# A graph network of three layers: the next layer's products over its first eight source pairs, dealt between the steps of a layer's last four tiles

## The chip, the cores and the metric

The kernel runs on one core of one Trainium2 chip, in one launch. The metric is the device time of a run in microseconds (us); less is better. The engines of the core work side by side, each through its own instructions in order: TensorE (PE, with PEld for its weight loads), VectorE (DVE), ScalarE (ACT), GpSimd (POOL) and SyncE (SP), which here only issues transfers. PE writes to PSUM, 16 DMA engines move the data.

## The reference

```python
src, dst = edge_index[0], edge_index[1]          # 200000 edges, sorted by dst
h = jnp.maximum(_layernorm(x, axis=-1), 0.0)     # x: 6250 x 128, float32

def _sage_conv(x, src, dst, Wl, bl, Wr):
    agg = jax.ops.segment_max(x[src], dst, num_segments=x.shape[0])
    agg = jnp.where(jnp.isfinite(agg), agg, 0.0)
    return agg @ Wl + bl + x @ Wr

h = jax.nn.leaky_relu(_sage_conv(h, src, dst, Wl1, bl1, Wr1), 0.01)   # 128 -> 256
h = jax.nn.leaky_relu(_sage_conv(h, src, dst, Wl2, bl2, Wr2), 0.01)   # 256 -> 256
h = jax.nn.leaky_relu(_sage_conv(h, src, dst, Wl3, bl3, Wr3), 0.01)   # 256 -> 128
return x + h
```

Each layer takes, for every node, the elementwise maximum over the rows of its in-edges' sources, and puts that and the node's own row through two products. Destinations are drawn with the square of a uniform number, so low node numbers have many edges and high ones few.

## The kernel before

**Tiles and pairs.** The nodes lie in 50 tiles of 127. As sources the tiles are taken two at a time: 25 pairs, `g` from 24 down to 0, a pair's features being 512 KB in layers 1 and 2 and 256 KB in layer 0 (the features stand there in two parts, whose products are summed). As destinations they are cut into five groups `k`: 0 has 24 narrow tiles (few edges), 1 has 11 wide tiles, 2 has 8 virtual tiles (the three tiles with the most edges, spread over more rows, with eight extra planes), 3 has 8 wide tiles, 4 has the last 4 narrow tiles.

**Products.** For a pair and a destination tile, one edge per destination row (wide tiles: one from each tile of the pair) is fetched by a product with a one-hot matrix. `one_hot` makes these on ACT: in layer 0 from the edge list (L916) and stores them in a compact form for later (`far`, L922), then the float form (L920); later layers load `far` and need only L920. `products` (L939) issues the PE work of a **step**, `maxima` (L954, L956) takes the result on DVE into an accumulator `acc` in SBUF. In layers 1 and 2 a step is four tiles of 128 columns: eight products of 512 columns on PE, and one maximum of 1024 elements per row on DVE for narrow tiles, two for wide ones. A source pair is six steps for group 0, three wide ones for group 1 (the third of 384 columns), two wide and two narrow ones for group 2, two wide ones for group 3 and one narrow one for group 4. In layer 0, with half the features, a step is eight tiles.

**Lists.** The edges that no one-hot serves stand in four lists. A list is worked off by **gathers** of 128 rows (`Listed.gather`, L988: an indirect DMA issued by POOL, and behind it a small memset L992 that spaces them), with an index made by ACT (`release`, L977) and the maxima on DVE (`maximum`, L1003 and L1008). `CAPS` has the gathers of each list: 147, 91, 228 and 47, 513 per layer. The last list belongs to group 4. Gathers of a layer read the table of all nodes' rows, so they start only when the last node of the layer before is done.

**Nodes.** A tile that has all its maxima becomes a `Node`: `fetch` (L1033, the list's result, an indirect DMA by POOL), `merge` (transposes on PE L1049, maximum on DVE L1055), `linear` (products L1060, L1062, L1064 on PE, copy L1066 on ACT), `rows` (L1073), `turn` (transposes of the new row block L846 to L851) and `rest` (L856). The virtual tiles first go through `Joined`: eight fetches, eight merges (L1112, L1114), a scan, eight `send`s (transposes L1124, copy L1126 into one buffer `joined_v`, a store), and then three nodes.

**Order.** Everything is written out by hand, step by step. A planner first lists the steps:

```python
PASSES = (((0,), (1,), (2,), (3,), (4,)), ((0, 1), (2, 3), (4,)), ((0, 1), (2, 3), (4,)))
```

so layer 0 goes through its groups one by one, 25 pairs each, and layers 1 and 2 have three passes over the pairs: groups 0 and 1 together (225 steps), groups 2 and 3 (150 steps), group 4 (25 steps). Then it puts every gather, maximum and node stage at a step of an `agenda`; in each step the stages of that step are issued between the two halves of its products. Gathers of lists 0 to 2 are spread evenly from the layer's first steps (`rows_at`) to the end of group 3, those of list 3 over the last pass. The nodes of groups 0 and 1 come at every third step of the second pass, those of group 3 and the virtual ones in the last pass, one per step, and the four of group 4 after it, in the next layer's first steps. The preparation of lists 1 to 3 and of the one-hots (`chores`: `mask_rows`, `flag_rows`, `pick_rows`, `rank_rows`, `expand`, `lookups`, all DVE) lies in steps 0 to 172 of layer 0. Pairs are loaded two orders ahead into three buffers (`load_pair`), one-hots are made up to six ahead (`make_hots`).

Of the kernel before, what the change touches and what calls it, by code (L numbers as in the profile page):

```python
# [42 lines left out]
P = 128  # L43
# [16 lines left out]
)  # L60
DEEP = (24, 24, 48, 24)
NA = 8
WINDOW = (48, 64)
# [6 lines left out]
def kernel(ctx: ExitStack, tc: tile.TileContext, x, src, dst,  # L70
# [33 lines left out]
    PASSES = (((0,), (1,), (2,), (3,), (4,)), ((0, 1), (2, 3), (4,)), ((0, 1), (2, 3), (4,)))  # L104
# [6 lines left out]
    LISTS = (GROUPS[0], GROUPS[1], GROUPS[2] + GROUPS[3], GROUPS[4])  # L111
# [32 lines left out]
    GB = (1, 1, 1, 1, 5)  # L144
# [802 lines left out]
    def maxima(step, s, p, acc):  # L947
        layer, k, g, (c, w, _, odd_u), _ = step
        if widths[layer] // P == 2:
            of, to = p[:, :, :w], acc[:, :, c * P : c * P + w]  # L950
        else:
            of, to = p.rearrange("p h c -> p (h c)")[:, :w], acc[:, 0, c * P : c * P + w]
        if g == NG - 1 and c == step[3][2] and (odd_u is None or s == 0):
            nc.vector.tensor_copy(to, of)  # L954
        else:
            nc.vector.tensor_max(to, to, of)  # L956
# [188 lines left out]
    steps, begins, ends_at, order, blocks, jobs_h = [], [], {}, [], [], []  # L1145
    for layer in range(3):
        begins.append(len(steps))
        for n, ks in enumerate(PASSES[layer]):
            for g in range(NG - 1, -1, -1):
                order.append((layer, n, g))  # L1150
                of = {}
                for k, (c0, pw, odd), cs in parts_in(layer, ks):
                    if k not in of:
                        if (NG - 1 - g) % GB[k] == 0:
                            blocks.append((layer, k, list(range(g, g - GB[k], -1))))
                        of[k] = max(i for i, b in enumerate(blocks) if b[:2] == (layer, k))
                    jobs_h += [(len(steps), of[k], (layer, k, g, c0, pw, odd, s)) for s in range(2)]
                    for c in cs:
                        steps.append((layer, k, g, c, n))
                        ends_at[layer, k] = len(steps)  # L1160
    begins.append(len(steps))
# [21 lines left out]
    EXTRA_OF = GROUPS[VIRT]  # L1183

    def late_rows(k):
        us = LISTS[k]
        i0 = 0
        for part in [[u for u in us if (u in EXTRA_OF) == v] for v in (True, False)]:
            if not part:
                continue  # L1190
            chores.append((2.5, lambda part=part: mask_rows(part, S_acc)))
            chores.append((18 if part[0][0] == "w" else 6, lambda part=part: flag_rows(part, S_acc)))
            for i in range(0, len(part), 4):
                chores.append((7, lambda k=k, i0=i0 + i, p=part[i : i + 4]: pick_rows(k, i0, p, S_acc)))
# [31 lines left out]
    stops.append((len(chores), 52, 104))  # L1226
    for s in range(2):
        late_lookups(GROUPS[3], s)
    stops.append((len(chores), 104, 140))
    late_rows(3)  # L1230
    late_lookups(LISTS[3], 0)
    stops.append((len(chores), 140, 172))
# [7 lines left out]
    i0 = 0  # L1240
# [8 lines left out]
    for layer in range(3):  # L1249
        b0, end = begins[layer], begins[layer + 1]  # L1250
        lists_ = [early_list if (layer, k) == (0, 0) else Listed(layer, k) for k in range(NL)]
        early = 0 if layer else EARLY
        turn = ends_at[layer, 3] - DELAY[layer]
        whens = []
        for part, t0, t1 in ((lists_[:3], max(b0 + 2, rows_at), turn), (lists_[3:], turn, end - 1 - SOON)):
# [23 lines left out]
        late = 0  # L1279
# [15 lines left out]
        free = 0  # L1295
        for k in range(len(GROUPS)):
            done = done_at[LISTED[GROUPS[k][0]][0]]
            n = len(GROUPS[k])
            if k == VIRT:
                t0 = joins = max(ends_at[layer, k], done + gap) + 1  # L1300
                key = (layer, "joined")

                def start(key=key, layer=layer):
                    accs[key] = Joined(layer, accs[layer, VIRT])

                plan(t0, MAXIMA, start)
                for v in range(NV):
                    plan(t0 + v, FETCH, lambda key=key, v=v: accs[key].fetch(v))
                    plan(t0 + 2 + v, MERGE, lambda key=key, v=v: accs[key].merge(v))
                for i in range(widths[layer] // P):  # L1310
                    plan(t0 + 10, MERGE, lambda key=key, i=i: accs[key].scan(i))
                for v in range(NV):
                    plan(t0 + 11 + v // 2, TURN, lambda key=key, v=v: accs[key].send(v))
                continue
            nodes = [
                ((layer, k, "node", i), lambda layer=layer, k=k, i=i: Node(layer, k, i, accs[layer, k]))
                for i in range(n - 1, -1, -1)
            ]
            if k == len(GROUPS) - 1:
                t0 = max(end, done + 1) + 1  # L1320
                assert free <= t0
                for j, (key, make) in enumerate(nodes):
                    stages(t0, key, make, after=[d + j for d in (2, 3, 3, 4)])
                rows_at = max(late, t0 + 3 + n - 1)
                continue
            t0 = max(ends_at[layer, k], done + gap, free) + 1
            every = 1 if layer == 0 or k == 3 else 3
            for j, (key, make) in enumerate(nodes):
                stages(t0 + every * j, key, make)
            free = t0 + every * (n - 1) + 1  # L1330
            if k == VIRT + 1:
                free = max(free, joins + 17)
                for a in range(VT):
                    stages(free + a, (layer, None, a), lambda layer=layer, a=a: Node(layer, None, a, None))
                free += VT
            late = max(late, free + 4)
# [36 lines left out]
    ACC = ((0, 0), (1, 8), (1, 0), (1, 19), (0, 20))  # L1373
# [3 lines left out]
    for t in range(max(max(agenda)[0] + 1, len(steps) + 1)):  # L1377
# [4 lines left out]
        if t == begins[1]:  # L1382
# [324 lines left out]
```

## Time and profile before

| | us |
|---|---|
| three timed runs | 3393.09, 3399.34, 3400.73 (median 3399.34) |
| the profiled execution's own time | 3386.89 |
| its span in the profile | 3384.8 |
| PE busy in the span | 2535.2 (75%) |
| DVE busy | 2674.5 (79%) |
| POOL busy | 2461.2 (73%) |
| ACT busy | 1879.2 (56%) |

The profile is one execution. A view by stretches of the span gives each engine's busy time, the granted clock of PE as a share of full speed, and what the DMA engines moved. A row of the timeline has the start, the time taken, the engine, line and operation, output and inputs, shape, a count, and in brackets the idle time before it and what ended it. The rows of a chain of waits have start, length and what it was. The boundaries between passes used below are the starts of the first product of each pass, found by counting the products of L939.

### The profile page before, as it was taken

To read this page: it belongs to the slowest core of one execution; us is meant where nothing else is said; L and a number is where in the kernel's file an instruction comes from. 1 tells how busy PE (TensorE), PEld (TensorE's weight loads), DVE (VectorE), ACT (ScalarE), POOL (GpSimd) and SP (SyncE) were. 2 spreads that over 40 slices of the span, in tenths; PEclk is the share of its full clock that TensorE was granted. 3 is DMA by queue.
4 is the path that set the end of the run, shared out by engine and by line. 5 is a ranking of instruction groups with operands and counts; after the bars stand their busy time and mean duration, and the time that the engine had idled before them with its cause. 6 is when DMAs were issued, how large, how long until landed. Compare 5 with 4: busy or idle time off the path is not lost.

```text
span 3384.8 us, 38792 instructions
## 1 busy us (share of the span) xinstructions
PE 2535.2 (75%) x9920; PEld 1833.9 (54%) x9920; DVE 2674.5 (79%) x4157; ACT 1879.2 (56%) x2762; POOL 2461.2 (73%) x3478
## 2 busy tenths in 40 slices
PE   1035664365676667899999989887999999989886
PEld 1023333243454333677777666655777777666654
DVE  6677679777766653699989888884699989999974
ACT  5128897466999996555544434433455545333432
POOL 4788865476867655488888767775388888878782
PEclk9986777587778876899999999998999999999998
DMA  9234554267676677656757767667666756666575
GB/s 303 50 65 135 140 140 134 82 199 195 164 223 172 191 210 206 187 183 199 195 175 187 225 201 226 203 190 241 210 194 194 202 176 179 203 188 206 171 228 166
DMA packets 355527, 620.98 MB, mean 183 GB/s; under 512 B 68694, under 2 KB 216883, under 8 KB 354657
## 3 DMA queue, kind: packets, MB, share of 16 engines
q1 hardware_dynamic: 210561, 367.36, 33.7%
q0 software_dynamic: 79872, 199.22, 24.1%
q10 hardware_dynamic: 64864, 51.83, 4.5%
q8 instruction: 83, 1.36, 0.2%
q14 instruction: 147, 1.20, 0.1%
HBM read 476.03 MB, written 142.13 MB: 183 GB/s over the span
## 4 chain that ended last, share of the span: by engine, by line
PE 28%; DVE 22%; POOL 16%; DMA 12%; issue 11%; ACT 10%; SPq 0%; ACTq 0%; DVEq 0%; POOLq 0%
PE pg L939 21%; DVE acc L956 10%; POOL g L988 9%; ACT away L916 6%; DMA g<-table,let 5%; POOL pace_t L992 3%; ACT hot L920 3%; DVE g L1008 2%; PE z_p L1062 2%; DVE g L1003 2%; PE z_p L1064 2%; POOL picks L621 2%; DMA far<-away 1%; DMA joined<-joined_v 1%; DVE acc L557 1%
## 5 line engine op out<-in xcount | busy, mean ns | idle before, releaser
L939 PE MATMUL pg<-hot,pair_sb 128*128 128x512 f32 x8000 | 2212.9, 426 | 425.3 <-ACT hot L920 191.3
L939 PEld LDWEIGHTS pg<-hot,pair_sb 128*128 128x128 f32 x8000 | 1551.0, 204 | 950.8 <-ACT hot L920 422.2
L988 POOL DMA_INDIRECT g<-table,let x1539 | 1552.1, 1009 | 664.5 <-ACT let L977 291.0
L956 DVE TENSOR_TENSOR acc<-acc,pg 128x1024 f32<-128x1024 f32 (+3 forms) x1439 | 1642.8, 1167 | 415.0 <-PE pg L939 388.7
L920 ACT ACTIVATE hot<-idx_sb 128x1024 fp32r<-128x1024 uint8 (+1 forms) x900 | 817.1, 946 | 552.7 <-PE pg L939 349.2
L992 POOL MEMSET pace_t<- 128x300 bf16 x1539 | 563.0, 366 | 0.8
L916 ACT ACTIVATE away<-idx_sb,near 128x1024 uint8<-128x1024 uint8 (+2 forms) x450 | 463.7, 1030 | 68.4 <-DMA best<-g 17.7
L920 ACT ACTIVATE hot<-away 128x1024 fp32r<-128x1024 uint8 (+2 forms) x450 | 427.7, 950 | 46.0 <-PE pg L939 31.8
L1066 ACT COPY s<-z_p 127x256 f32<-127x256 f32 (+1 forms) x150 | 50.2, 334 | 452.0 <-PE z_p L1064 421.0
L1003 DVE TENSOR_TENSOR g<-g 128x1024 f32<-128x1024 f32 (+5 forms) x218 | 221.4, 1016 | 20.4 <-DMA g<-table,let 20.2
L1033 POOL DMA_INDIRECT agg<-best,end_i x141 | 144.7, 1026 | 106.9 <-PE aT_p L1049 41.2
L1008 DVE TENSOR_TENSOR g<-g 128x512 f32<-128x512 f32 (+3 forms) x351 | 173.1, 493 | 10.5 <-DMA g<-table,let 0.2
L1062 PE MATMUL z_p<-wr,hT_in 128*128 128x256 f32 (+1 forms) x500 | 142.9, 404 | 6.6 <-DMA hT_in<-across 6.6
L1064 PE MATMUL z_p<-wl,mz 128*128 128x256 f32 (+1 forms) x500 | 127.7, 373 | 14.6 <-DVE mz L1055 13.8
L846 PE MATMUL hT_p<-ident,h 128*128 128x128 f32 x200 | 47.9, 326 | 116.2 <-DVE mz L1055 54.1
L977 ACT ACTIVATE let<-ell 128x4 int32<-128x4 int16 (+3 forms) x444 | 81.1, 191 | 79.1 <-DMA ell<-picks 67.7
L848 ACT COPY hT<-hT_p 128x254 f32<-128x254 f32 x100 | 36.7, 367 | 141.5 <-PE hT_p L846 136.6
L1064 PEld LDWEIGHTS z_p<-wl,mz 128*128 128x128 f32 x500 | 91.8, 212 | 32.4 <-DVE mz L1055 22.3
L846 PEld LDWEIGHTS hT_p<-ident,h 128*128 128x128 f32 x200 | 24.6, 158 | 148.2 <-DVE mz L1055 67.1
L1062 PEld LDWEIGHTS z_p<-wr,hT_in 128*128 128x128 f32 x500 | 82.1, 207 | 31.4 <-issue 8.9
L1055 DVE TENSOR_TENSOR mz<-acc,aT_p 128x256 f32<-128x256 f32 (+1 forms) x141 | 52.3, 371 | 58.4 <-PE aT_p L1049 58.3
L621 POOL DMA_INDIRECT picks<-picked,to_i x55 | 57.7, 1050 | 43.0 <-DVE rank_h L597 32.6
(268 smaller groups left out, 1223.2 us busy)
## 6 DMA issues: line engine op xcount, KB each, us to landing
pair_sb<-pair SPq DMA_DIRECT2D x150, 512.0 KB
far<-away ACTq DMA_DIRECT2D x350, 128.0 KB
idx_sb<-far SPq DMA_DIRECT2D x50, 768.0 KB
pair_sb<-pair SPq DMA_DIRECT2D x125, 256.0 KB
pair<-pr SPq DMA_DIRECT2D x100, 256.0 KB
idx_sb<-far SPq DMA_DIRECT2D x50, 512.0 KB
g<-table,let POOLq DMA_INDIRECT x1539
idx_sb<-idx SPq DMA_DIRECT2D x50, 384.0 KB
```

What stands on the lines that cost most here:

```text
L621: s = nc.gpsimd.indirect_dma_start(out=picks[k], out_offset=bass.IndirectOffsetOnAxis(ap=to_i[k][:, i : i + 1], axis=0), in_=picked[k][:, ...
L916: nc.scalar.activation(away, t[:, at : at + w], AF.Abs, bias=near[:, s : s + 1], scale=1.0)
L920: nc.scalar.activation(hot[:, :w], away, AF.Relu, bias=1.0, scale=-1.0)
L939: nc.tensor.matmul(to, pr[:, s, i, kk * P : (kk + 1) * P], hot[:, o : o + bw], start=((alone or s == 0) and i == 0), stop=((alone or s == ...
L956: nc.vector.tensor_max(to, to, of)
L988: nc.gpsimd.indirect_dma_start(out=self.tiles[q, b][:, i, :], out_offset=None, in_=tables[self.layer], in_offset=bass.IndirectOffsetOnAxis ...
L992: nc.gpsimd.memset(pace_t, 0.0)
L1003: nc.vector.tensor_max(base[:, : i + 1, :], base[:, : i + 1, :], g[:, : i + 1, :])
L1008: nc.vector.tensor_max(base[:, :h, :], base[:, :h, :], base[:, w - h : w, :])
L1033: nc.gpsimd.indirect_dma_start(out=self.agg[:, : self.F], out_offset=None, in_=of, in_offset=bass.IndirectOffsetOnAxis(ap=at, axis=0),)
L1062: nc.tensor.matmul(z_p, self.hT[:, i, :], wr[layer][:, i, :], start=False, stop=False)
L1064: nc.tensor.matmul(z_p, self.m[:, i, :], wl[layer][:, i, :], start=False, stop=(i == K - 1))
```

## The change

The last pass of layers 0 and 1 is no longer 25 steps of group 4: between them stand the six group-0 steps of the next layer for each of its first eight source pairs, 48 steps, so that the pass has 73. The pairs 24 to 17 are concerned, whose tiles are nodes of group 0 and are done earlier in the layer. The next layer's first pass then starts with group 0 alone for two more pairs (`MORE`), 12 steps, goes on with groups 0 and 1 for the 15 pairs left, and the second pass takes group 1 along for the first ten pairs (9 steps a pair), then groups 2 and 3 for 15 (6 steps a pair). Group 4's accumulator moves to the place of group 1's.

With it change: the lists (list 3 now has half of group 3 and group 4, 98 gathers instead of 47; list 2 has 182 instead of 228; 518 per layer); in layer 2 all four lists are spread evenly to the end of the last pass; the nodes of groups 0 and 1 come at every fourth step in layers 1 and 2, four nodes of group 3 and the three virtual ones at every third; the other four nodes of group 3 come with those of group 4 after the last pass, eight instead of four; group 4's one-hot inputs are loaded pair by pair instead of five pairs at once; and the chores for list 3 stand earlier, all chores ending at step 156.

```diff
-    (47, 24, 20, 17, 16, 15, 14, 13, 12, 12, 11, 10, 8, 6, 2, 1),
-    (23, 10, 8, 6),
+    (47, 24, 19, 17, 15, 14, 13, 12, 10, 8, 2, 1),
+    (31, 15, 12, 11, 9, 8, 7, 5),
 )
-DEEP = (24, 24, 48, 24)
+DEEP = (24, 24, 48, 32)
+OVER, MORE = 8, 2
...
-    LISTS = (GROUPS[0], GROUPS[1], GROUPS[2] + GROUPS[3], GROUPS[4])
+    LISTS = (GROUPS[0], GROUPS[1], GROUPS[2] + GROUPS[3][:4], GROUPS[3][4:] + GROUPS[4])
...
-    GB = (1, 1, 1, 1, 5)
+    GB = (1, 1, 1, 1, 1)
...
+    back, walks = list(range(NG - 1, -1, -1)), []
     for layer in range(3):
+        if layer == 0:
+            body = [(n, g, (k,)) for n, k in enumerate((0, 1, 2, 3)) for g in back]
+        else:
+            late_g = back[: OVER + MORE]
+            body = [(0, g, (0,)) for g in back[OVER : OVER + MORE]] + [(0, g, (0, 1)) for g in back[OVER + MORE :]]
+            body += [(1, g, (1, 2, 3) if g in late_g else (2, 3)) for g in back]
+        walks += [(layer, *w) for w in body]
+        last = [((i + 0.5) / NG, layer, 4, g, (4,)) for i, g in enumerate(back)]
+        if layer < 2:
+            last += [((i + 0.6) / OVER, layer + 1, 0, g, (0,)) for i, g in enumerate(back[:OVER])]
+        walks += [w[1:] for w in sorted(last)]
...
+        spans = ((lists_[:3], begin_at, turn), (lists_[3:], turn, end - 1 - SOON))
+        if layer == 2:
+            spans = ((lists_, begin_at, end - 1 - SOON),)
...
+        every = 1 if layer == 0 else 4
+        for k in (0, 1):
+            for i in range(len(GROUPS[k]) - 1, -1, -1):
+                t = max(t, ready(k, i))
+                stages(t, *node_of(k, i))
+                t += every
...
+        t0 = max(t, end, done_at[3] + 1) + 1
+        lasts = [(4, i) for i in range(3, -1, -1)] + [(3, i) for i in range(7, 3, -1)]
+        for j, (k, i) in enumerate(lasts):
+            f = max(0, j - 2)
+            stages(t0 + f, *node_of(k, i), after=[d + j - f for d in (2, 3, 3, 4)])
...
-    ACC = ((0, 0), (1, 8), (1, 0), (1, 19), (0, 20))
+    ACC = ((0, 0), (1, 8), (1, 0), (1, 19), (1, 8))
...
-        if t == begins[1]:
+        if t == done_with_fields:
             making.close()
             fields.close()
```

More of the change, by code (lines that the diff above doesn't have):

```diff
@@ L1143, in parts_in @@
         return [p[1:] for p in sorted(parts, key=lambda p: p[:2])]
-    steps, begins, ends_at, order, blocks, jobs_h = [], [], {}, [], [], []
+    steps, begins, ends_at, order, blocks, jobs_h = [], {}, {}, [], [], []
+    back, walks = list(range(NG - 1, -1, -1)), []
     for layer in range(3):
[L1147 to L1160, printed above, removed]
@@ new lines @@
+        if layer < 2:
+            last += [((i + 0.6) / OVER, layer + 1, 0, g, (0,)) for i, g in enumerate(back[:OVER])]
+        walks += [w[1:] for w in sorted(last)]
+    first_g = {}
+    for layer, n, g, ks in walks:
+        order.append((layer, n, g))
+        of = {}
+        for k, (c0, pw, odd), cs in parts_in(layer, ks):
+            first_g.setdefault((layer, k), g)
+            if k not in of:
+                blocks.append((layer, k, [g]))
+                of[k] = len(blocks) - 1
+            jobs_h += [(len(steps), of[k], (layer, k, g, c0, pw, odd, s)) for s in range(2)]
+            for c in cs:
+                begins.setdefault(layer, len(steps))
+                steps.append((layer, k, g, c, n))
+                ends_at[layer, k] = len(steps)
@@ L1181, with runs_of @@
     here_now, listed_at = [0], {0: 0}
-    EXTRA_OF = GROUPS[VIRT]
+    def runs_of(us):
+        cuts = [i for i in range(1, len(us)) if us[i] != (us[i - 1][0], us[i - 1][1] + 1)]
+        return list(zip([0] + cuts, cuts + [len(us)]))
     def late_rows(k):
@@ L1293, in stages @@
                 plan(ta + d, rank, lambda stage=stage: getattr(accs[key], stage)())
[L1295 to L1336, printed above, removed]
@@ new lines, in ready, with node_of @@
+        def ready(k, i):
+            return max(ends_at[layer, k], done_at[LISTED[GROUPS[k][i]][0]] + gap) + 1
+        def node_of(k, i):
+            return (layer, k, "node", i), lambda layer=layer: Node(layer, k, i, accs[layer, k])
+        t = 0
+        every = 1 if layer == 0 else 4
[4 more added lines that the diff above has]
+                t += every
+        assert t + 5 < ends_at[layer, VIRT]
@@ new lines, with start @@
+        joins = max(ready(VIRT, 0), t)
+        key = (layer, "joined")
+        def start(key=key, layer=layer):
+            accs[key] = Joined(layer, accs[layer, VIRT])
+        plan(joins, MAXIMA, start)
+        for v in range(NV):
+            plan(joins + v, FETCH, lambda key=key, v=v: accs[key].fetch(v))
+            plan(joins + 2 + v, MERGE, lambda key=key, v=v: accs[key].merge(v))
+        for i in range(widths[layer] // P):
+            plan(joins + 10, MERGE, lambda key=key, i=i: accs[key].scan(i))
@@ new lines @@
+        for v in range(NV):
+            plan(joins + 11 + v // 2, TURN, lambda key=key, v=v: accs[key].send(v))
+        every = 3
+        for i in range(3, -1, -1):
+            t = max(t, ready(3, i))
+            stages(t, *node_of(3, i))
+            t += every
+        t = max(t, joins + 17)
+        for a in range(VT):
+            stages(t, (layer, None, a), lambda layer=layer, a=a: Node(layer, None, a, None))
+            t += every
+        t0 = max(t, end, done_at[3] + 1) + 1
+        lasts = [(4, i) for i in range(3, -1, -1)] + [(3, i) for i in range(7, 3, -1)]
```

31 lines of the change are left out of this document (16 added, 15 removed).

## The prediction, on record before the changed kernel ran

> **What bounds the kernel now.** First the page, for the whole span:
>
> ```profile
> span 3384.8 us, 38792 instructions
> PE 2535.2 (75%) x9920; PEld 1833.9 (54%) x9920; DVE 2674.5 (79%) x4157; ACT 1879.2 (56%) x2762; POOL 2461.2 (73%) x3478
> PEclk9986777587778876899999999998999999999998
> ```
>
> No engine is full, and the clock is low only in the first 40%, layer 0. These are means over stages, so next the view by stretches, cut at the passes: layer 0's group 3 and group 4, then for layer 1 and layer 2 each the steps in which the last nodes of the layer before end (9 steps), the rest of the first pass (24 pairs), the second pass (25 pairs), the last pass (25 steps), and the tail.
>
> ```profile
> core 0: us, PE busy (x) PEld busy (x) DVE busy (x) ACT busy (x) POOL busy (x), PEclk, DMA share, GB/s
> 1147.60:1257.30 109.70, 75.37 (x201) 42.92 (x201) 70.75 (x73) 106.96 (x117) 67.29 (x101) 0.81 0.76 212
> 1257.30:1374.80 117.50, 77.78 (x203) 41.78 (x202) 42.18 (x88) 75.18 (x145) 59.90 (x79) 0.63 0.69 193
> 1374.80:1402.20 27.40, 26.18 (x109) 19.30 (x108) 18.26 (x27) 15.11 (x30) 1.30 (x2) 0.90 0.62 204
> 1402.20:1835.40 433.20, 406.00 (x1730) 321.11 (x1729) 396.42 (x398) 225.56 (x325) 379.68 (x553) 0.98 0.63 188
> 1835.40:2271.20 435.80, 389.36 (x1656) 287.57 (x1655) 386.42 (x426) 186.84 (x313) 321.12 (x451) 0.98 0.69 206
> 2271.20:2393.10 121.90, 93.02 (x375) 67.05 (x375) 62.73 (x84) 40.42 (x94) 63.41 (x80) 0.89 0.76 249
> 2393.10:2425.50 32.40, 28.87 (x128) 22.05 (x127) 18.56 (x25) 15.12 (x29) 1.36 (x3) 0.95 0.53 186
> 2425.50:2855.40 429.90, 402.80 (x1729) 319.01 (x1728) 396.34 (x398) 225.65 (x325) 377.94 (x553) 0.99 0.64 190
> 2855.40:3254.00 398.60, 356.23 (x1586) 263.60 (x1585) 376.07 (x426) 159.12 (x243) 321.92 (x451) 0.98 0.65 190
> 3254.00:3358.40 104.40, 79.95 (x354) 58.03 (x353) 60.80 (x85) 31.23 (x72) 60.90 (x79) 0.90 0.75 239
> 3358.40:3384.80 26.40, 9.83 (x48) 8.04 (x48) 5.29 (x16) 1.06 (x4) 1.89 (x2) 0.66 0.23 61
> ```
>
> In the first passes PE is busy 94% and DVE 92%; in the second passes both 89% to 94%. Only the last passes have room on DVE (51% of 121.9, 36% of 117.5), and there PE is still busy 93.02 of 121.9. Layer 0 is ACT's (106.96 of 109.7). So the 48 moved steps are to be priced by PE and DVE where they leave, and by PE where they arrive. Then the rows that price single pieces:
>
> ```profile
> 1398.43 11.21 PE L939 MATMUL pg<-hot,pair_sb 128*128 128x512 f32 x48
> L956 DVE TENSOR_TENSOR acc<-acc,pg 128x1024 f32<-128x1024 f32 x485 | 577.1, 1217 | 81.2 <-PE pg L939 71.9
> L956 DVE TENSOR_TENSOR acc<-acc,pg 128x768 f32<-128x768 f32 x48 | 45.6, 950 | 1.7
> ...
> 2505.05 0.95 POOL L988 DMA_INDIRECT g<-table,let  x1 [0.16 <-issue]
> 2506.00 0.36 POOL L992 MEMSET pace_t<- 128x300 bf16 x1
> 2506.53 0.95 POOL L988 DMA_INDIRECT g<-table,let  x1 [0.16 <-issue]
> ...
> L1033 POOL DMA_INDIRECT agg<-best,end_i x36 | 37.9, 1054 | 6.1 <-issue 5.6 <-PE z_p L1064 0.2 <-DVE g L1003 0.2
> ```
>
> A product of 512 columns is 11.21/48 = 0.234 us, a narrow step (eight) 1.87 us of PE and 1.22 of DVE; a wide step 1.87 of PE and 2.43 of DVE. So narrow steps are PE's, wide ones DVE's, and the mix of six and three keeps both near full. A gather takes POOL 1.48 us from start to start when nothing holds it: the 271 gathers planned in 1402.2:1835.4 are 401 of 433 us. Node stages and their waits, in one step of the last pass (PE's timeline):
>
> ```profile
> 2302.73 0.38 PE L846 MATMUL hT_p<-ident,h 128*128 128x128 f32 x2
> 2302.86 1.17 PE L939 MATMUL pg<-hot,pair_sb 128*128 128x512 f32 x4
> 2303.96 0.28 PE L1060 MATMUL z_p<-bias,ones_b 3*128 3x256 bf16 x1
> ...
> 2306.00 0.38 PE L1112 MATMUL vT_p<-ident,agg_v 128*128 128x128 f32 x2
> 2307.26 0.44 PE L1049 MATMUL aT_p<-ident,agg 128*128 128x128 f32 x2 [0.88 <-DVE acc L1114]
> 2307.46 1.18 PE L939 MATMUL pg<-hot,pair_sb 128*128 128x512 f32 x4
> ...
> 2330.54 0.69 PE L846 MATMUL hT_p<-ident,h 128*128 128x128 f32 x2 [3.12 <-ACT joined_v L1126]
> 2342.33 0.44 PE L846 MATMUL hT_p<-ident,h 128*128 128x128 f32 x2 [3.71 <-ACT joined_v L1126]
> 2350.97 0.69 PE L846 MATMUL hT_p<-ident,h 128*128 128x128 f32 x2 [3.61 <-ACT joined_v L1126]
> ```
>
> From start to next start a node is 0.13 + 2.04 + 0.20 = 2.37 us of PE, a joined merge 1.26 with its wait. The sends hold PE, which is in order, 10.4 us. So the last pass is not empty time: its steps are PE work of nodes, and its holes are round trips inside PE's own order, which other products placed around them do not fill.
>
> **The change, part by part.** Counts are of the steps and agenda that the code writes.
>
> *Last pass of layer 1, 73 steps.* PE: 73 x 1.87 = 137, seven nodes 17, eight joined merges 10, sends' own transposes 4, together 168; sends' waits 10 and some 8 of other waits as before (121.9 - 93.02 is 29 in all, pairs included). A group-4 step uses a whole pair of 512 KB; the load two orders ahead starts when the buffer of the pair before is free. The chain of waits shows how long that takes:
>
> ```profile
> 2360.27 5.59 DMA pair_sb<-pair
> 2369.23 4.35 DMA pair_sb<-pair
> 2375.63 6.68 DMA pair_sb<-pair
> ```
>
> 5.5 us on average. Group-4 steps now stand in threes: the third waits 5.5 - 2 x 1.87 = 1.8 us, in eight places 15. Sum 168 + 10 + 8 + 15, about 203 (between 168, no wait left, and 220): **+81** on 121.9. The 48 steps (90 us) thus come almost at full price.
>
> *Last pass of layer 0, 73 steps.* Here ACT is the limit, and PE work can lie under it:
>
> ```profile
> L916 ACT ACTIVATE away<-idx_sb,near 128x512 uint8<-128x512 uint8 x49 | 35.0, 714 | 5.4 <-DMA far<-away 5.4
> L920 ACT ACTIVATE hot<-away 128x512 fp32r<-128x512 uint8 x49 | 30.9, 630 | 1.6
> L920 ACT ACTIVATE hot<-idx_sb 128x1024 fp32r<-128x1024 uint8 x2 | 2.1, 1063 | 0.0
> 1374.52 0.66 PE L846 MATMUL hT_p<-ident,h 128*128 128x128 f32 x2 [10.43 <-DVE h L1073]
> ```
>
> ACT: 50 x (0.714 + 0.630) = 67 for group 4 and 48 x 1.063 = 51 for the moved one-hots, 118, and some 20 for nodes and sends. PE: 484 products 113, nodes at most 17, joined work 14, waits of sends 10: 154. The granted clock of this pass is 0.63, that of the dense passes 0.98, and the 27.4 us behind it have 0.90; I take full speed, since 48 dense steps arrive in runs of six (11 us). At 0.63 the 113 would be 179 and the pass 220. The Trainium skill, page "TensorE: Matmul & The Clock Gate", section "Part 1: The HAM clock gate (the "warmup" mystery)", has the clock halved after an idle window of about 3.4 us and full again after a busy one; by that rule the value is 154, not 220, and the rows 0.63 and 0.98 agree with it. So 154: **+37**. The 10.43 us wait for the later layers' weights moves behind the pass.
>
> *The 12 steps after each last pass* end eight nodes instead of four: 22.5 + 8 x 2.37 = 41.5. After layer 0 with the 10.43 and 2 of waiting 54 for 27.4, **+27**; after layer 1 with the 6 of waiting that 32.4 - 9 x 1.87 - 4 x 2.37 leaves, 48, **+16**.
>
> *Layer 1's other passes.* First pass 15 pairs instead of 24, at 433.2/24 = 18.05: 271. Second pass: as before 435.8, and for ten pairs three wide steps, of DVE 4 x 1.217 + 2 x 0.950 = 6.77 each pair, with 48 more gathers (396.42 less 24 x 14.1 of maxima is 59 for 271, 0.22 each): 78 of DVE, at this pass's 386.42/435.8 it is 88. 271 + 524 = 795 for 869: **-74**. Not 102 for the 51 steps gone, because those were PE's and what stays together is DVE's.
>
> *Layer 2's other passes.* The same on DVE: 15 x 17.91 and 398.6 + 83. But its 518 gathers now start at step 684 of 1025 and not 632, and are spread evenly: 199 fall into the 15 pairs, 199 x 1.48 = 295 where the steps need 269; 290 into the second pass, with 36 fetches at 1.2 472 for 482. I take 300 + 488 = 788 for 828.5: **-40** (POOL alone would allow 767).
>
> *Layer 2's end.* Four nodes fewer in the last pass, -8; four more in the tail with nothing beside them, about 3 each: **+4**. *Layer 0 before its last pass*: 46 fewer gathers, but ACT sets the pace, and the chores are the same within 30 small DVE instructions: **0** (-15 to +10). Group 4's single index loads are 128 KB for 640 KB per five pairs, the same bytes.
>
> Sum: 81 + 37 + 27 + 16 - 74 - 40 + 4 = **+51 us**. The profiled execution took 3386.89 us, so 3438; the median of the timed runs lies 12.5 above it, and 3399.34 + 51 is **3450**.
>
> **The rivals.** *Idle is filled (faster).* Stretches with different limits are mixed, and each ends up as full as the first passes are. The last passes take PE's work without waits, 168 and 144, at 0.94: 179 and 153 (+57, +36). The second pass takes the ten pairs' wide steps at PE's price, 16 products and 8 of three quarters, 5.2 a pair, 52 in all: -110 in layer 1, and -61 in layer 2, where POOL's 767 stops it. With +27, +16 and +4 that is -31: 3368. It decides from where those wide steps cost under some 6 us a pair, not 8.8 and 8.3. For it: DVE is half idle in the last passes. Against: DVE would be busy 464 of 488 us in layer 1's second pass, 95%, where it has 89% now. The Trainium skill, page "Perfetto Trace Analysis", section "Optimization Strategy", says that a kernel whose most contended engine changes over time may gain by interleaving its regimes; by that rule this rival holds, and the stretches above bear it out for layer 0's last pass alone, where ACT stands against PE.
>
> *The clock stays low.* Layer 0's last pass takes 220: +117, 3516. Against it: the 0.90 just behind.
>
> *POOL paces layer 2.* At the 433.2/271 = 1.60 us per gather of now, 489 gathers and 36 fetches take 825: -3 for -40, +88 in all, 3487. For it: nothing in that pass has been seen faster.
>
> *The price is kept everywhere*: a step costs the same in both places, within 7 us of 3399.
>
> **How the numbers follow.** Forecast 0.48, idle filled 0.22, clock low 0.12, POOL 0.13, price kept 0.05. About 0.2% (7 us) is what a measurement of this kernel can tell from no change. Faster 0.22, same 0.05, slower 0.48 + 0.12 + 0.13 = 0.73. The forecast's own ends are 3410 (layer 1's last pass at 168 and the list of small terms as taken) and 3490 (220 there, and half of what POOL or the clock would add). The range goes down to 3360, which takes in over half of the first rival, and up to 3515, with POOL's and half of the clock's: some 0.15 is left out.
>
> **What would show it.** Right: last passes near 154 and 203 us; in the second passes DVE as busy as now and PE less; POOL at 1.48 back to back through layer 2's first pass; waits of PE for pair_sb at every third group-4 step. Wrong: last passes under 145 and 180, a second pass of layer 1 under 490, or PE's clock in layer 0's last pass still near 0.63.

## The result, and the profile after

The changed kernel takes 3441.02 us (median of four runs, 3439.08 to 3441.91), the kernel before 3398.54 us beside it (four runs, 3393.09 to 3400.73): a ratio of 1.0127, 95% interval 1.0109 to 1.0144, so 42 us slower. The forecast was 3450, the range 3360 to 3515. The profiled execution took 3441.43 us, 54.5 more than the one before, which was 11.7 us under its kernel's median; the sum had said 51. Its page begins:

```profile
span 3439.6 us, 38911 instructions
PE 2544.1 (74%) x9920; PEld 1828.8 (53%) x9920; DVE 2674.8 (78%) x4182; ACT 1876.4 (55%) x2768; POOL 2477.2 (72%) x3508
PEclk9997887676788789899999999999999999999987
```

Busy times are those of before within 20 us on every engine: the same work, arranged so that it takes 55 us more. The view by stretches of the changed kernel, cut at the starts of the passes as before: layer 0's group 0 and group 1; its last pass and the 12 steps behind; layer 1's first pass, its second pass in two halves of 90 steps, its last pass and the 12 steps behind; layer 2's first pass and the two halves of its second.

```profile
core 0: us, PE busy (x) PEld busy (x) DVE busy (x) ACT busy (x) POOL busy (x), PEclk, DMA share, GB/s
236.70:600.50 363.80, 221.99 (x635) 137.66 (x636) 290.42 (x738) 329.37 (x359) 249.82 (x378) 0.78 0.51 138
600.50:879.40 278.90, 169.42 (x524) 112.49 (x522) 217.86 (x520) 183.86 (x297) 172.19 (x250) 0.70 0.61 169
1220.30:1413.20 192.90, 149.98 (x557) 109.27 (x557) 101.90 (x134) 121.97 (x202) 127.74 (x181) 0.87 0.62 179
1413.20:1459.60 46.40, 38.16 (x161) 26.45 (x160) 25.33 (x45) 19.60 (x39) 7.56 (x8) 0.93 0.65 207
1459.60:1732.80 273.20, 251.50 (x1081) 198.66 (x1081) 247.06 (x250) 141.69 (x207) 239.59 (x351) 0.99 0.63 186
1732.80:2005.50 272.70, 236.25 (x1008) 179.06 (x1006) 239.87 (x276) 109.21 (x200) 208.72 (x293) 0.96 0.67 195
2005.50:2253.30 247.80, 216.01 (x891) 158.44 (x890) 224.10 (x235) 105.66 (x169) 185.50 (x266) 0.98 0.64 195
2253.30:2444.70 191.40, 163.83 (x708) 125.78 (x707) 129.94 (x139) 90.07 (x150) 129.51 (x179) 0.97 0.76 241
2444.70:2490.00 45.30, 44.59 (x202) 32.38 (x202) 23.63 (x36) 18.84 (x38) 7.58 (x8) 1.00 0.69 218
2490.00:2790.70 300.70, 261.39 (x1081) 203.47 (x1080) 254.91 (x261) 142.43 (x213) 266.44 (x389) 0.96 0.61 176
2790.70:3056.60 265.90, 216.81 (x964) 157.88 (x964) 238.42 (x276) 94.78 (x161) 233.83 (x329) 0.96 0.65 180
3056.60:3301.10 244.50, 206.61 (x865) 148.42 (x864) 225.71 (x242) 95.45 (x146) 215.46 (x306) 0.97 0.64 183
```

Layer 0's first two groups were, in the view by stretches of the kernel before:

```profile
236.70:637.70 401.00, 223.97 (x635) 143.34 (x636) 315.89 (x824) 328.28 (x365) 275.71 (x409) 0.71 0.48 128
637.70:912.60 274.90, 162.21 (x525) 108.28 (x524) 203.81 (x402) 183.53 (x299) 199.71 (x283) 0.74 0.65 177
```

Two readings carry the result. **Where the steps arrive**: layer 0's last pass grew by 75.4 us (117.5 to 192.9) and PE's busy time in it by 72.2 (77.78 to 149.98); layer 1's grew by 69.5 and PE's busy time by 70.8. PE idles 42.9 and 27.6 us in them, where it idled 39.7 and 28.9. The dealt steps hardly went into the holes; they stand beside them. In layer 1 PE's waits for `joined_v`, the round trips of the sends, are 12.4 us before and 9.1 after. In layer 0 the 10.43 us wait that ended this pass in the kernel before is gone from it, and 11.8 us of waits for pairs have come. **Where they left**: layer 1's first and second pass together shrank by 75.3 (869.0 to 793.7), though PE's work there shrank by 91.6 (795.4 to 703.8). What the time follows is DVE's work, 782.8 to 711.0: 90% of the time before, 90% after.

### The profile page after: what moved, and what is told of

Read it like the earlier page. It is cut to its first block, busy times and chain, and to the rows that moved or that the text cites. A ratio compares the mean times of both kernels' runs of the same rounds, so it can differ in the third digit from the quotient of the medians.

```text
span 3439.6 us, 38911 instructions
## 1 busy us (share of the span) xinstructions
PE 2544.1 (74%) x9920; PEld 1828.8 (53%) x9920; DVE 2674.8 (78%) x4182; ACT 1876.4 (55%) x2768; POOL 2477.2 (72%) x3508
## 4 chain that ended last, share of the span: by engine, by line
PE 24%; DVE 21%; POOL 17%; DMA 15%; issue 11%; ACT 11%; SPq 1%; DVEq 0%; ACTq 0%; POOLq 0%
PE pg L939 18%; POOL g L988 11%; DVE acc L956 11%; ACT away L916 6%; DMA g<-table,let 4%; POOL pace_t L992 4%; ACT hot L920 3%; DMA agg<-best,end_i 2%; PE z_p L1062 2%; DVE g L1008 2%; DVE g L1003 2%; DMA pair_sb<-pair 2%; PE z_p L1064 1%; DMA far<-away 1%; POOL picks L621 1%
## 5 line engine op out<-in xcount | busy, mean ns | idle before, releaser
L939 PE MATMUL pg<-hot,pair_sb 128*128 128x512 f32 (+1 forms) x8000 | 2232.3, 428 | 459.5 <-ACT hot L920 197.8
L939 PEld LDWEIGHTS pg<-hot,pair_sb 128*128 128x128 f32 x8000 | 1553.8, 205 | 995.7 <-ACT hot L920 407.4
L956 DVE TENSOR_TENSOR acc<-acc,pg 128x1024 f32<-128x1024 f32 (+3 forms) x1439 | 1642.3, 1166 | 442.8 <-PE pg L939 421.5
L1003 DVE TENSOR_TENSOR g<-g 128x1024 f32<-128x1024 f32 (+5 forms) x223 | 225.2, 1010 | 51.1 <-DMA g<-table,let 46.2
L1008 DVE TENSOR_TENSOR g<-g 128x256 f32<-128x256 f32 (+3 forms) x351 | 173.0, 493 | 13.5 <-DMA g<-table,let 3.3
L846 PEld LDWEIGHTS hT_p<-ident,h 128*128 128x128 f32 x200 | 22.8, 153 | 153.7 <-DVE mz L1055 61.4
L1062 PEld LDWEIGHTS z_p<-wr,hT_in 128*128 128x128 f32 x500 | 82.0, 207 | 28.9 <-issue 6.2
L1049 PE MATMUL aT_p<-ident,agg 128*128 128x128 f32 x250 | 58.7, 302 | 50.6 <-DMA agg<-best,end_i 43.5
```

Of the source, the lines that this page charges most:

```text
L939: nc.tensor.matmul(to, pr[:, s, i, kk * P : (kk + 1) * P], hot[:, o : o + bw], start=((alone or s == 0) and i == 0), stop=((alone or s == ...
L1003: nc.vector.tensor_max(base[:, : i + 1, :], base[:, : i + 1, :], g[:, : i + 1, :])
L1008: nc.vector.tensor_max(base[:, :h, :], base[:, :h, :], base[:, w - h : w, :])
L1062: nc.tensor.matmul(z_p, self.hT[:, i, :], wr[layer][:, i, :], start=False, stop=False)
```

## The experiments

Each kernel was timed in turn with the kernel before on one chip. That kernel's medians were 3398.54 us beside the changed kernel, 3438.20 beside the first four experiments, then 3390.23, 3460.22 and 3393.49, so between these sets only ratios are compared, and stretches with care. The sets are over_none to before_cost, before_again to over_half, joined_spread to before_load_late, and dealt_three. Stretches are from one profiled execution each, cut at the first product (L939) of each pass; "+ steps" are the 9 steps (kernels with the old end) or 12 behind a last pass, "other" the first and second pass less these.

| kernel | ratio (95%) | setup | layer 0, groups 0-3 | last | + steps | layer 1, other | last | + steps | layer 2, other | end |
|---|---|---|---|---|---|---|---|---|---|---|
| before | 1 | 236.7 | 1020.6 | 117.5 | 27.4 | 869.0 | 121.9 | 32.4 | 828.5 | 130.8 |
| changed | 1.0127 (1.0109-1.0144) | 236.7 | 983.6 | 192.9 | 46.4 | 793.7 | 191.4 | 45.2 | 811.2 | 138.6 |
| over_none | 1.0011 (0.9992-1.0031) | 261.1 | 1021.6 | 86.4 | 45.5 | 885.6 | 110.6 | 44.7 | 842.3 | 145.1 |
| over_first | 1.0069 (1.0046-1.0092) | 263.7 | 987.4 | 193.5 | 47.7 | 832.5 | 101.8 | 44.7 | 845.0 | 141.6 |
| over_second | 1.0110 (1.0067-1.0153) | 264.7 | 1017.5 | 85.2 | 45.2 | 865.0 | 194.9 | 45.1 | 801.0 | 142.2 |
| before_cost | 1.0008 (0.9988-1.0029) | 264.8 | 1024.4 | 122.1 | 29.7 | 869.2 | 124.6 | 32.6 | 832.6 | 137.5 |
| before_again | - | 237.6 | 1019.4 | 115.1 | 29.6 | 873.5 | 121.5 | 32.7 | 832.1 | 131.6 |
| after_again | 1.0128 (1.0090-1.0165) | 235.8 | 985.5 | 197.5 | 46.8 | 793.3 | 195.1 | 45.7 | 802.0 | 139.7 |
| fetch_early | 1.0131 (1.0093-1.0170) | 234.8 | 980.6 | 186.8 | 47.4 | 791.4 | 201.8 | 45.5 | 800.3 | 145.1 |
| over_half | 1.0103 (1.0066-1.0141) | 233.7 | 984.2 | 157.8 | 45.8 | 816.2 | 169.8 | 46.2 | 827.2 | 137.4 |
| joined_spread | 1.0067 (1.0047-1.0087) | 267.4 | 997.7 | 185.0 | 47.4 | 792.2 | 189.2 | 44.9 | 808.1 | 145.9 |
| none_three | 0.9964 (0.9947-0.9981) | 274.1 | 1025.5 | 86.3 | 45.5 | 871.8 | 106.3 | 44.8 | 848.8 | 143.2 |
| before_load_late | 0.9988 (0.9968-1.0007) | 266.3 | 1021.1 | 120.2 | 29.8 | 874.5 | 125.7 | 32.4 | 837.9 | 141.1 |
| dealt_three | 1.0074 (1.0052-1.0096) | 236.6 | 976.4 | 181.9 | 46.4 | 792.3 | 184.3 | 45.2 | 803.1 | 143.9 |

**Is it the dealing, and which boundary?** One edit of the changed kernel gives four kernels, (0, 0), (8, 0), (0, 8) and (4, 4):

```diff
-OVER, MORE = 8, 2
+OVERS, MORE = (0, 0), 2
...
+            OVER = OVERS[layer - 1]
             late_g = back[: OVER + MORE]
...
-            last += [((i + 0.6) / OVER, layer + 1, 0, g, (0,)) for i, g in enumerate(back[:OVER])]
+            last += [((i + 0.6) / OVERS[layer], layer + 1, 0, g, (0,)) for i, g in enumerate(back[: OVERS[layer]])]
...
-        if layer == 2:
+        if layer == 2 or not OVERS[layer]:
             spans = ((lists_, begin_at, end - 1 - SOON),)
```

A boundary without dealing differs from the changed kernel in one more thing: the gathers of its layer are spread evenly to the end of the last pass. It also keeps `MORE = 2`, so group 1's steps for the first two pairs stay in the second pass; the kernel before has them in the first.

> The changed kernel with no dealing at either boundary: each last pass is 25 steps of group 4 again, the next layer's first pass has all 25 pairs (two with group 0 alone). The new lists, the new places of their preparation, the eight end nodes and the single index loads stay; all four lists are spread evenly in every layer. Theory on record (the dealt steps cost nearly full price where they arrive, 75 + 19 and 69 + 13 us in the traces, and give back 75 and 17 where they leave): without them 3441 - 84 = about 3357, between 3345 and 3375, and layer 0's first pass keeps the 37 us that it won, since that comes from the preparation. Rival (dealing fills idle time, and the lists and end nodes are what costs): 3441 or more.

> Dealing at the boundary of layers 0 and 1 alone. Theory: +75 in layer 0's last pass, +19 behind it, -75 in layer 1's other passes, so 19 above the kernel without dealing, 3376 (3366 to 3390). Rival of the prediction on record for this place (ACT's time in layer 0's last pass hides PE's work, idle is filled): at or below the kernel without dealing.

> Dealing at the boundary of layers 1 and 2 alone. Theory: +69 in layer 1's last pass, +13 behind it, -17 in layer 2's other passes, so 65 above the kernel without dealing, 3422 (3410 to 3432): this boundary carries most of the loss, because layer 2 gives back only 17. Rival (both boundaries cost the same): 42 above, about 3399.

Without dealing the kernel is as fast as the one before (1.0011), so the loss goes with the dealing; the lists, the end nodes and the single index loads cost nothing in sum that the interval shows. The spread of the gathers changes with the dealing here; over_half below has the changed kernel's spread with half of the dealing. That the kernel without dealing would be 42 us faster than the one before (3357) fell. The boundaries cost 20 us (3459.76 less 3440.18) and 31 (3471.56 less the same): the first as expected (19), the second half of the theory's 65 and under the rival's 42 too, but with five runs and an interval of 15 us to each side. In the traces, the first boundary adds 75 us from layer 0's first product to the end of its nodes (1228.6 for 1153.5) and gives 62 back in layer 1 (979.0 for 1040.9); the second adds 64 (1105.0 for 1040.9) and gives 44 back (943.2 for 987.4).

The view by stretches of over_none: layer 0's last pass, layer 1's second and last, layer 2's second. The stretches of second passes shown here and further down begin 4 to 5 us, two steps, behind the pass's first product.

```profile
1282.60:1369.10 86.50, 62.85 (x157) 33.48 (x157) 33.85 (x67) 71.76 (x132) 54.19 (x79) 0.70 0.82 237
1838.10:2300.20 462.10, 394.94 (x1687) 294.57 (x1688) 398.36 (x437) 188.02 (x321) 348.35 (x491) 0.98 0.68 199
2300.20:2410.80 110.60, 80.53 (x310) 57.77 (x309) 53.27 (x67) 35.01 (x76) 42.90 (x54) 0.86 0.74 243
2879.70:3297.90 418.20, 363.78 (x1618) 269.00 (x1619) 388.94 (x437) 160.76 (x251) 349.43 (x490) 0.98 0.66 186
```

Its layer 0 shows where the 37 us went that the theory counted on. Group 0 keeps its gain (365.2 us), but with even lists group 1 takes 293.7 us where over_first, on the same chip, takes 276.8, and group 3, in whose pass `Joined` now begins, 122.9 for 107.3. So groups 0 to 3 take 1021.6 us again; the last pass takes 86.5 instead of 117.5, the eight end nodes 45.5 for 27.4.

**Do the first dealt pairs cost less?**

> The changed kernel with four source pairs dealt at each boundary instead of eight: 24 steps in each last pass. Theory (each dealt step costs about the same, since PE's own work and its round trips fill these passes already): half of the loss, a ratio of 1.005 to 1.009. Rival (the first steps fill idle time, only the later ones cost): 1.003 or less, or a gain. Second rival (most of the loss comes with the first dealt pairs, by the lists and pair loads that go with them): 1.010 or more.

1.0103, which is the second rival's figure (1.010 or more), with an interval that reaches from half of the changed kernel's loss (1.0064), the theory's, to all of it. That the first steps are free is excluded; theory and second rival are not told apart. By the table 24 steps make the last passes 43 and 48 us longer than in before_again, on the same chip, and the next 24 another 40 and 25 (after_again). In these two the spread of the gathers is the same, and the other 24 steps cost 15.6 us by the medians (3420.25 and 3435.83), less than the intervals of the two ratios leave certain. Whether the price per step falls stays open.

**Layer 0's 37 us.** Two kernels are the kernel before with one line changed, and one is that kernel again:

```diff
-                chores.append((7, lambda k=k, i0=i0 + i, ...: pick_rows(...)))
+                chores.append((1.2 * (DEEP[k] // 4), lambda k=k, i0=i0 + i, ...: pick_rows(...)))
```

```diff
-        chores.append((0, load))
+        chores.append((0, lambda: plan(here_now[0] + 4, MAXIMA, load)))
```

> The kernel before with one number of the change: the cost that the planner gives to each pick_rows call, 7, becomes 1.2 per quarter of DEEP (7.2 for lists 1 and 3, 14.4 for list 2). The load of list 1 moves from step 18 to 19, list 2's preparation spreads over steps 52 to 80. Theory (layer 0's first pass won its 37 us by where the preparation stands, not by having 18 gathers and one pick_rows fewer): the 13 us wait at step 20 goes, and a good part of the other 24, so 3365 to 3385. Rival (it is the smaller list 2 and the fewer gathers): 3395 to 3400, no difference.

> The kernel before, unchanged, for a second profile of it. Question: are the 37 us by which layer 0's first pass was shorter in the profile after a property of the change, or do single profiled executions differ by that much? Theory A (it belongs to the change): the first pass of layer 0 takes 395 to 405 us again and the wait of 13 us at step 20 is there again. Theory B (it is one execution's stalls): 365 to 385, near the 375 of the kernel with the new cost of pick_rows and the 363 to 367 of the three kernels with the new lists.

> The kernel before with the load of each finished list (ell from picks, issued by SP) four steps later. In the kernel before SP stands at this load from 330 to 350 us, since POOL is still fetching picks, and a load of the next pair stands behind it: PE waits 13 us at step 20. Theory (part of the 37 us of layer 0's first pass is this wait, which the changed kernel avoids because its list 0 is gathered more slowly and the picks end 4 us earlier): step 20 takes 5 us, groups 0 and 1 of layer 0 together 650 to 665 us for 676, a ratio of 0.994 to 0.998. Rival (the time is ACT's and DVE's backlog and comes back some steps later): a ratio of 0.999 to 1.002.

The kernel before took 399.8 us for group 0 again, so the 37 are no chance of one execution. With the new cost, group 0 takes 375.3 and group 1 306.6 where it had 274.9: moved, not won. With the late load, SP's timeline first of the kernel before, then of before_load_late:

```profile
330.31 0.37 SPq L885 DMA_DIRECT2D idx_sb<-idx  x1
350.23 0.32 SPq L631 DMA_DIRECT2D ell<-picks  x1
350.64 0.38 SPq L896 DMA_DIRECT2D pair_sb<-pair  x1
```

```profile
364.56 0.16 SPq L896 DMA_DIRECT2D pair_sb<-pair  x1
372.84 0.32 SPq L631 DMA_DIRECT2D ell<-picks  x1
```

Before, SP stands 20 us at the load of list 1, and the next pair's load behind it; PE's step 20 takes 17.5 us. With the pair's load ahead of it step 20 takes 4.3, but list 2's load does the same at step 80 (22.8 us for 6.2), and groups 0 and 1 take 676.1 us for 675.9. So neither is the cause; the rivals held. All ten executions with the new lists took 362 to 367 us for group 0: the gain comes with what they bring. Which part (list 2 with 12 rows for 16, one `pick_rows` less, or slower gathering) was not separated. The traces point to the preparation on DVE: in group 0 DVE's work fell from 315.9 to 290.4 us, of which 14.1 came back in group 1, and PE's wait for the ranks of the lists (L581) fell from 21.2 to 6.0 us.

**Layer 2's second pass.**

```diff
-                stages(t, *node_of(k, i))
+                stages(t, *node_of(k, i), after=(11, 12, 13, 14) if layer == 2 else (3, 4, 5, 6))
```

> The changed kernel, unchanged, on the chip of this call, for its ratio and a second profile. Theory (the two dealings cost 20 and 34 us by the medians and the rest of the change nothing): a ratio of 1.011 to 1.017, the last passes of layers 0 and 1 again 190 to 196 us each. Rival (the first ratio was its chip's): under 1.008.

> The changed kernel with one edit in layer 2: the nodes of groups 0 and 1 have their other stages 8 steps later, so that the fetch by POOL stands 11 steps ahead of the merge that uses it instead of 3. Theory (layer 2's second pass took 506 to 510 us for a forecast of 488 because POOL, late with 518 gathers, issues these fetches late, and PE, in order, waits 37.4 us for them): the wait for agg falls under 10 us, the second pass to 475 to 492, the whole 15 to 30 us below the changed kernel, a ratio to before of 1.004 to 1.008. Rival (the pass is POOL's or DVE's anyway, and the wait only shows who is last): the wait turns into waits of PE for maxima, the time stays within 7 us of the changed kernel.

The ratio of the changed kernel is confirmed. The views of waits (PE's) and of stretches for layer 2's second pass, first of after_again, then of fetch_early:

```profile
PE pg L939 <- DVE acc L956: 44.8, 63, 2.3
PE aT_p L1049 <- DMA agg<-best,end_i: 23.5, 11, 10.8
```

```profile
2804.60:3301.70 497.10, 417.31 (x1810) 301.97 (x1811) 459.36 (x513) 187.84 (x302) 437.02 (x623) 0.97 0.64 182
```

```profile
PE pg L939 <- DVE acc L956: 58.3, 64, 3.3
```

```profile
2790.50:3288.50 498.00, 425.31 (x1809) 313.40 (x1810) 459.68 (x513) 188.21 (x303) 438.40 (x622) 0.95 0.64 182
```

The wait for fetches is gone, that for maxima grew by 13.5, and the pass is as long as before. DVE is busy 459 of 497 and 498 us: the wait only showed which of PE's waits ended last, as the rival had it. My theory fell. Whether POOL, busy 437 and 438 us, holds a part of this pass was not separated.

**The waits in the last passes.** The view of waits of the changed kernel in layer 0's last pass (us in total, times, longest) has for PE:

```profile
PE pg L939 <- DMA pair_sb<-pair: 11.8, 7, 3.8
PE pg L939 <- ACT hot L920: 7.7, 5, 2.2
PE vT_p L1112 <- DMA agg_v<-best,end_i: 7.4, 4, 5.2
PE jT_p L1124 <- ACT joined_v L1126: 6.0, 5, 3.4
...
PE hT_p L846 <- ACT joined_v L1126: 2.3, 2, 1.6
```

```diff
-            plan(joins + v, FETCH, ... fetch(v))
-            plan(joins + 2 + v, MERGE, ... merge(v))
+            plan(joins + (2 * v if wide else v), FETCH, ... fetch(v))
+            plan(joins + (2 * v + 3 if wide else v + 2), MERGE, ... merge(v))
...
-            plan(joins + 11 + v // 2, TURN, ... send(v))
+            plan(joins + (20 + 2 * v if wide else 11 + v // 2), TURN, ... send(v))
...
-        t = max(t, joins + 17)
+        t = max(t, joins + (37 if wide else 17))
```

> The changed kernel with the work of Joined spread over the longer last passes of layers 0 and 1: its eight fetches and merges at every second step (each merge three steps behind its fetch), its eight sends one at every second step instead of two per step, the three virtual nodes behind them, so that this work fills some 50 of the 73 steps instead of 32. Theory (the last passes lose time in PE's own order: 15.7 us of waits for agg_v and joined_v in layer 0, 10.5 in layer 1, and dealt steps between a send and the next would cover them): these waits fall under 6 us in all, the two passes become 15 to 25 us shorter together, a ratio of 1.006 to 1.009 where the changed kernel has 1.013. Rival (the waits are only the form of a pass that is held by pair loads, one-hots and PE's products): other waits grow, within 7 us of the changed kernel.

Its two last passes, and PE's largest wait in each:

```profile
1265.00:1450.10 185.10, 147.49 (x557) 108.00 (x558) 100.97 (x134) 122.33 (x202) 126.72 (x181) 0.87 0.67 187
2289.70:2478.90 189.20, 165.79 (x708) 128.66 (x707) 129.60 (x139) 88.36 (x150) 127.23 (x180) 0.96 0.78 244
```

```profile
PE pg L939 <- DMA pair_sb<-pair: 16.4, 8, 3.0
...
PE pg L939 <- DMA pair_sb<-pair: 13.5, 8, 3.7
```

PE's waits for agg_v and joined_v are no longer among the rows, and the passes together take 374 us where the changed kernel's two executions took 384 and 393. The ratio, 1.0067, is what the theory expected; since the two were not timed on one chip, how much of the step from 1.0127 is this edit's is known by the intervals only. The waits for pair_sb stay: three group-4 steps in a row use up three pairs.

**No dealing, other spacing of nodes; and both repairs with dealing.** none_three is over_none with these lines, dealt_three the changed kernel with these and those of joined_spread:

```diff
-        every = 1 if layer == 0 else 4
+        every = 1 if layer == 0 else 3
...
+                stages(t, *node_of(k, i), after=(8, 9, 10, 11) if layer else (3, 4, 5, 6))
```

> The kernel without dealing, with the nodes of groups 0 and 1 in layers 1 and 2 at every third step as in the kernel before, and their fetch 8 steps ahead of the merge. Question: why are the second passes of layers 1 and 2 there 462 and 418 us, where the kernel before has 436 and 399. Theory (the spacing of four: PE waits 40 us for rows where it waited 25, and 14 us for fetches): 436 to 445 and 400 to 410, a ratio of 0.990 to 0.994, which would beat both kernels. Rival (DVE sets these passes, busy 398 and 389 us with 20 more gathers each): only a few us, a ratio of 0.997 to 1.001.

> The changed kernel with both repairs: the work of Joined spread over the longer last passes, and the nodes of groups 0 and 1 in layers 1 and 2 at every third step with their fetch 8 steps ahead. Question: is the loss of the dealing only the order of the node work around it, or the dealt steps themselves. The kernel without dealing and with the second of these repairs had 0.9964. Theory (48 PE-bound steps bring some 90 us of PE into a pass that PE sets, and take less than that from passes that DVE sets): a ratio of 1.000 to 1.006, above 0.9964 whatever is done around it. Rival (with the round trips covered, idle time is filled): 0.997 or less.

none_three is a little faster than both kernels: 0.9964, interval 0.9947 to 0.9981. That lies between the theory (up to 0.994) and the rival (from 0.997). Its second passes say why it is no more:

```profile
1856.00:2303.10 447.10, 398.88 (x1687) 293.72 (x1688) 398.87 (x437) 191.31 (x321) 348.81 (x490) 0.98 0.73 206
2876.30:3303.00 426.70, 367.78 (x1617) 265.93 (x1618) 389.19 (x437) 163.85 (x251) 350.92 (x494) 0.98 0.66 183
```

Layer 1's is 15 us shorter than in over_none; layer 2's is 9 longer, which stays unexplained. DVE has more work there than in the kernel before. Counted from the pass's first product, layer 1's has 403.3 us of it in 451.6, where the kernel before has 386.4 in 435.8. Of these 17 us, by the view of groups of lines, 9.4 are maxima into `acc` (L956), since `MORE` keeps six wide steps of group 1 in this pass, and 6.7 are gathers' maxima (L1003, L1008), which the even lists put there. `MORE = 0` was not run. dealt_three has 1.0074, a little above the theory's 1.006: with its round trips spread, the dealt kernel still loses, and PE is busy 148.59 of 182.0 and 163.88 of 184.3 us in its last passes:

```profile
1213.00:1395.00 182.00, 148.59 (x557) 109.17 (x558) 100.99 (x134) 122.77 (x202) 126.90 (x181) 0.88 0.67 190
2233.70:2418.00 184.30, 163.88 (x708) 127.75 (x707) 129.59 (x139) 88.46 (x150) 127.06 (x178) 0.97 0.80 250
```

## Why the prediction was right, and where it was wrong

The reason held: the last passes are PE's work and PE's round trips, so PE-bound steps cost there nearly what they take, and the passes that they leave are DVE's (layer 2's first POOL's) and give back less. The kernels without dealing show that the loss goes with the dealing and not, in sum, with the lists or the end nodes; the spread of the gathers, which changes with it there, was not switched alone. The first rival, that idle is filled, fell with PE's idle time nearly unchanged in amount. It was to hold where the ten pairs' wide steps cost under 6 us a pair in the second pass; layer 1's grew by 84.7 us (435.8 to 520.5), 8.5 a pair, against the 8.8 of the forecast. That the price is kept everywhere, within 7 us, fell by the 42 us. Beside it: the Trainium skill's advice on interleaving regimes (page "Perfetto Trace Analysis", section "Optimization Strategy") does not carry over here, since the moved steps lean on PE and the stretch that takes them has its room on DVE; dealt_three is 1.0074 with it, none_three 0.9964 without.

The terms against the profiled execution:

| term | forecast | measured |
|---|---|---|
| layer 1's last pass | +81 | +69.5 |
| layer 0's last pass | +37 | +75.4 |
| steps behind layer 0, layer 1 | +27, +16 | +19.0, +12.8 |
| layer 1's other passes | -74 (271 and 524) | -75.3 (273.2 and 520.5) |
| layer 2's other passes | -40 (300 and 488) | -17.3 (300.7 and 510.4) |
| layer 2's end | +4 | +7.8 |
| layer 0 before its last pass | 0 | -37.0 |
| sum | +51 | +54.8 |

**Layer 0's last pass was mis-sized.** The step that failed is "waits of sends 10" as the only wait, on the ground that ACT is the limit and hides PE. ACT was busy 122.0 of 192.9 us, so it was not the limit. PE's work was near enough, 150 us for 144. But PE waits 43 us, of which the view names 35: 11.8 for pairs, which I had counted for layer 1 (15) and not here though the same three group-4 steps stand together; 7.7 for one-hots; 7.4 for agg_v; 8.3 for the sends. The low clock of before did not stay: the granted clock rose from 0.63 to 0.87, and PE's busy time is only 6 us over the sum at full speed, where the second rival had the pass at 220 us; the Trainium skill's rule of the clock gate (page "TensorE: Matmul & The Clock Gate", section "Part 1: The HAM clock gate (the "warmup" mystery)") agrees in direction.

**Layer 0 before it was priced at 0 and gave 37.** That step failed too: "ACT sets the pace, and the chores are the same". The row behind it was group 3's alone (106.96 of 109.7). ACT was busy 328 us in group 0 before and 329 after, but idled 73 of 401.0 us before and 34 of 363.8 after: it did not set the pace all the time. Nor were DVE's chores in group 0 the same: DVE has 738 instructions there for 824 and 25.5 us less work. That the shorter time comes from this is argued, not shown. The two errors, 38 and 37 with opposite signs, cancelled: the sum was right in part by luck. Toggling the first boundary alone shows it: it costs 13 us in the traces and 20 by the medians, where +37 and -74 of the forecast made it a gain of 37 (the +27 behind the pass is the end nodes', which over_none has too).

**Layer 2 gave back 17 and not 40.** The first pass came as worked out (300.7 for 300), and by the mechanism: POOL is busy 266.4 us in it, and 29.5 more go by between one gather and the next ("issue" in its view of waits), so its gathers stand back to back. DVE waits 21.8 us for gathers to land there, and none in the kernel before: this pass goes by POOL, not by DVE. The second was too low by 22: I took DVE at the 94% of before, and it was busy 464.1 of 510.4 us, 91%. Two more executions took 802.0 and 800.3 for both passes, -30 against before_again's 832.1, so some of the miss is one execution's. POOL as the pace, the third rival, would have given -3. Layer 1's last pass, +69.5 for +81, had 8.0 us of pair waits where 15 were counted.

## What to carry to other kernels

Before work is moved between stretches with different limits, compare not how busy each is but which engine the moved piece needs and which engine sets each stretch: a PE step taken out of a DVE-bound pass frees less than its own time, and put beside PE's round trips it pays nearly full price. Holes that are waits inside one engine's own order are filled only by placing work between a request and its answer, not by adding work to the pass. And a right sum is no proof of its terms: switch each part off alone.

## What the runs showed of the hardware that was not expected

The same kernel took 3390 to 3460 us (medians) on different chips. In the profiles 23 to 40 us of such a difference lie before the first product of layer 0: 234 to 238 us on some, 261 to 274 on others, with the same work. And the granted clock of a pass depends on what stands in it: 0.63 for layer 0's last pass before, 0.78 in over_half, 0.87 with 48 dealt steps. The 48 steps of 1.87 us, 90, added only 72 us of PE's busy time there: four nodes, 9.5, left the pass, and a product of L939 took 629 ns on average before and 442 after.
